# A GRU with a mixture of experts behind it: two gates in one PSUM bank, made by matmuls of 256 columns

## The chip, the core and the metric

The kernel runs on one core of a Trainium2 chip. Its time is the device time of one execution in microseconds (us); lower is better. The runs before the change took 1448.86, 1452.12 and 1456.24 us, so the median is 1452.12 us. One further execution was recorded by the hardware profiler; it took 1449.96 us, and all readings of the profile below are of that execution. Engines are named as in the profile: PE is TensorE's matmul, PEld its weight load, DVE is VectorE, ACT is ScalarE, POOL is GpSimd, SP is SyncE.

## What is computed

`x` is (8, 256, 512): 8 sequences of 256 steps with 512 features. A GRU runs over the steps, and its states go through a mixture-of-experts layer; `x` is added at the end. Everything is float32.

```python
def cell(h, x):                       # h: (8, 512), once for each of 256 steps
    gi = x @ W_ih + b_ih              # W_ih, W_hh: (512, 3 * 512)
    gh = h @ W_hh + b_hh
    i_r, i_z, i_n = jnp.split(gi, 3, axis=-1)
    h_r, h_z, h_n = jnp.split(gh, 3, axis=-1)
    r = jax.nn.sigmoid(i_r + h_r)
    z = jax.nn.sigmoid(i_z + h_z)
    n = jnp.tanh(i_n + r * h_n)
    h_new = (1.0 - z) * n + z * h
    return (h_new, h_new)
...
# the states of all steps, as 2048 tokens
topk_w, topk_ids = jax.lax.top_k(softmax(tokens @ w_gate), 2)     # 8 experts, weights normed
routed = sum over the two chosen experts of  w * (silu(g) * u) @ w_down[e]
shared = (silu(g) * u) @ w_sh_down                                # for every token
out = x + routed + shared
```

## The kernel before

**Blocks and steps.** The 256 steps are 16 blocks (`NB`) of `TS` = 16 steps. Step `n` needs the state of step `n - 1`, so the recurrence is a chain of 256 steps. TensorE's other work is cut into pieces and put between the steps: the projections of `x` for later blocks (`project`, tile `gip`), the shared expert for blocks that are done (`shared_unit`, tiles `gu_s` and `po`), and the routing. The routed experts (`tile_unit`) come behind the last step, when it is known which tokens each expert has.

**One step (`step`).** A gate's values lie as 4 groups of 8 partitions (8 sequences each), with 128 columns. Three PSUM banks, `ps_r`, `ps_n` and `ps_z`, hold one gate each in their first 128 columns. A bank is first filled ("opened", `open_gate`, line 458) by ScalarE: it copies the input's share of the gate, which lies ready in `seeds` or `seeds_n`, into the bank. The matmuls then add `h @ W_hh` to it (line 478): for each gate 4 row blocks `q` of the state times 4 column groups `j`, 16 matmuls of 128 columns each. A float32 matmul stands in the profile as two passes, so a gate is 32 of them.

VectorE turns each gate by a transpose of 32x32 squares (`turned`, line 489), which also moves it out of PSUM. The order of the work of one step is the order of the lines:

- VectorE turns r; ScalarE takes its sigmoid (line 493) and opens r's bank for the next step (458);
- VectorE turns n and multiplies (496); ScalarE opens n's bank (458); VectorE adds the input's share of n (498); ScalarE takes the tanh (500);
- VectorE turns z; ScalarE takes its sigmoid (502) and opens z's bank;
- VectorE makes the new state in three operations (505, 507, 508), the last of which (`hT`) is what the next step's matmuls wait for; ScalarE keeps a copy of the state (511).

Every engine runs its own instructions in the order in which they are written. The waits between engines are set by a framework from the tiles that an instruction reads and writes.

**What stands between the steps.** After each step the loop over `t` calls the routing work that is due, then `catch_up(room)`, which runs work for VectorE from the list `afterwards` as far as 1.1 us (`WINDOW`) reach, and then takes pieces for TensorE from `queue` until the step's share of the block's work is done.

**x's turn.** `load_x(k)` brings a block of x by 8 loads on SP. `transpose_x(k)` turns it on VectorE (line 313) into `xT` for the projections and loads the next block behind that. Its place is set in the list of projections: a piece without work, put behind the projection of gate number 1 of a block, puts the turn of the next block into `afterwards`:

```python
for g in range(3):
    projections.extend(project(k, g))
    if g == 1 and k + 1 < NB:
        projections.append(Piece(lambda _: None, lambda k=k: turn_x_afterwards(k + 1), parts=0))
```

If a projection comes up before its turn has been run, the turn is run at once. Six pieces of this list are run before step 0, and `catch_up` behind them.

After the last step the three banks serve as `spare` for transposes of the routed experts.

Of the kernel before, what the change touches and what calls it, by code (L numbers as in the profile page):

```python
# [9 lines left out]
F32 = mybir.dt.float32  # L10
# [7 lines left out]
P = 128  # L18
# [7 lines left out]
def kernel(  # L26
# [52 lines left out]
    nc = tc.nc  # L79
    B, T, D = x.shape  # L80
# [4 lines left out]
    NQ = D // P  # L85
    NB = T // TS
# [16 lines left out]
    ps_gru = ctx.enter_context(tc.tile_pool(name="ps_gru", bufs=1, space=PSUM))  # L103
# [32 lines left out]
    whh = we[:, E - 4 : E - 2].rearrange("p e w n -> p (e w n)").rearrange("p (q n) -> p q n", q=NQ)  # L136
# [56 lines left out]
    seeds = [const.tile([P, SC, 2 * P], F32, name=f"seeds_{i}") for i in range(NS)]  # L193
# [6 lines left out]

    banks = {g: ps_gru.tile([P, D], F32, name=f"ps_{g}") for g in "rnz"}
    for bank in banks.values():
        nc.tensor.matmul(
            bank[:, 0:P], seeds[0][:, 0, 0:P], seeds[0][:, 0, 0:P], start=True, stop=True
        )
    xT_of = {}

    def turn_x_plain(k):  # L210
# [29 lines left out]
    def counting(name, n, base, step, channel):  # L240

        i = const.tile([P, n], I32, name=f"{name}_i")
        nc.gpsimd.iota(i, [[step, n]], base=base, channel_multiplier=channel)
        f = const.tile([P, n], F32, name=name)
        nc.vector.tensor_copy(f, i)
        return f
# [143 lines left out]
    def project(k, g):  # L390

        box = {}

        def issue(q, cols):
            if q == 0 and cols.start == 0:
                if k in turned_x:
                    turned_x.pop(k)()
                box["ps"], _ = bank_of([P, D], f"gip_{k}_{g}")
            multiply(
                box["ps"][:, cols],  # L400
                lambda c: xT_of[k][:, c, q, :],
                wih[:, q, g * D + cols.start : g * D + cols.stop],
                start=(q == 0 and cols.start == 0),
                stop=(q == NQ - 1 and cols.stop == D),
            )

        def by_group(t_):
            return t_.rearrange("p (q j i) -> p j q i", q=NQ, j=4)

        def end():  # L410
            to_gi = gi[:, :, g, :].rearrange("p j (q i) -> p j q i", q=NQ)
            bias_g = by_group(bias[:, g * D : (g + 1) * D])
            if k == 0:
                nc.vector.tensor_tensor(to_gi, by_group(box["ps"]), bias_g, ALU.add)
            else:
                nc.scalar.copy(to_gi, by_group(box["ps"]))
                nc.gpsimd.tensor_tensor(to_gi, to_gi, bias_g, ALU.add)
            if g > 0:
                to = gi_dram[k][g % 2].rearrange("j b t n -> (b t) j n")
                projected.add((k, "rzn"[g]))  # L420
                by = nc.sync if k else nc.scalar
                if g == 1:
                    by.dma_start(to.rearrange("p j (a n) -> p j a n", a=2), gi[:, :, 0:2, :])
                else:
                    by.dma_start(to, gi[:, :, 2, :])

        return [
            matmul_piece(lambda cols, q=q: issue(q, cols), end if q == NQ - 1 else None)
            for q in range(NQ)
        ]  # L430
# [4 lines left out]
    def load_seeds(c, of="nz"):  # L435

        k, o = divmod(c * SC, TS)
        steps = slice(o, o + SC)
        for g in of:
            assert (k, g) in projected  # L440
            tile_, at_row, src = (
                (seeds_n[c % NS], B, gi_dram[k][0]) if g == "n" else (seeds[c % NS], 0, gi_dram[k][1])
            )
            for j in range(4):
                by = nc.sync if c else nc.scalar
                row = 32 * j + at_row
                by.dma_start(tile_[row : row + B], src[j, :, steps, :])

    def open_gate(n, g):

        if n >= T:
            return
        c, t = divmod(n, SC)
        if g == "n":
            src = seeds_n[c % NS][:, t]
        else:
            src = seeds[c % NS][:, t].rearrange("p (a n) -> p a n", a=2)[:, "rz".index(g)]
        nc.scalar.copy(banks[g][:, 0:P], src)  # L458

    whh_v = whh.rearrange("p q (a k j i) -> p q a j k i", a=3, k=NQ, j=4)  # L460
    hc_of = {}

    def hc_of_block(k):
        return hc_of[k // 2][:, NG * (k % 2) : NG * (k % 2) + NG]
# [5 lines left out]
    def step(n):  # L470
        k, t = divmod(n, TS)
        c, ts = divmod(n, SC)
        hT, new = states[n % NH], states[(n + 1) % NH][:, :, 0:B]
        for g, bank in banks.items():
            a = "rzn".index(g)
            for q in range(NQ):
                for j in range(4):
                    nc.tensor.matmul(  # L478
                        bank[32 * j : 32 * j + B, 0:P].rearrange("b (k i) -> b k i", k=NQ),
                        hT[:, q, 0:B],  # L480
                        whh_v[:, q, a, j, :],
                        start=False,
                        stop=(q == NQ - 1),
                        skip_group_check=True,
                    )

        def turned(g):
            gT = turned_gates[g]
            nc.vector.transpose(gT.rearrange("p a b -> p (a b)"), banks[g][:, 0:P])  # L489
            return gT  # L490

        r = turned("r")[:, :, 0:B]
        nc.scalar.activation(r, r, AF.Sigmoid)  # L493
        open_gate(n + 1, "r")
        nT = turned("n")
        nc.vector.tensor_tensor(r, nT[:, :, 0:B], r, ALU.mult)
        open_gate(n + 1, "n")
        nc.vector.tensor_tensor(r, nT[:, :, B : 2 * B], r, ALU.add)  # L498
        nn = r
        nc.scalar.activation(nn, nn, AF.Tanh)  # L500
        z = turned("z")[:, :, 0:B]
        nc.scalar.activation(z, z, AF.Sigmoid)
        open_gate(n + 1, "z")

        nc.vector.tensor_tensor(hn, hT[:, :, 0:B], nn, ALU.subtract)  # L505
        nc.gpsimd.tensor_copy(last_hn, hn[:, 0, 0:1])  # L506
        nc.vector.tensor_tensor(z, z, hn, ALU.mult)
        nc.vector.tensor_tensor(new, nn, z, ALU.add)  # L508
        if t == 0 and k % 2 == 0:
            hc_of[k // 2] = two.tile([P, 2 * NG, NQ, 32], F32, tag="hc", name=f"hc_{k // 2}")  # L510
        nc.scalar.copy(  # L511
            hc_of_block(k).rearrange("p g q (c t) -> p q g c t", t=TS)[:, :, :, :, t],
            new.rearrange("p q (g c) -> p q g c", c=2),
        )
# [406 lines left out]
    for k in range(1, NB):  # L921
        for g in range(3):
            projections.extend(project(k, g))
            if g == 1 and k + 1 < NB:
                projections.append(
                    Piece(lambda _: None, lambda k=k: turn_x_afterwards(k + 1), parts=0)
                )

    def turn_x_afterwards(k):
        turned_x[k] = afterward(1.1, lambda: transpose_x(k))  # L930
# [3 lines left out]
        projections.popleft().run(None)  # L934
    catch_up(None)
    load_seeds(1)
    for g in banks:
        open_gate(0, g)
    for k in range(NB):

# [38 lines left out]
        for t in range(TS):  # L979
            n = k * TS + t  # L980
            step(n)
            if (n + 1) % SC == 0 and n + 1 < T and (n + 1) // SC + NS - 1 < T // SC:
                load_seeds((n + 1) // SC + NS - 1)
            room = WINDOW
            for cost, busy, work in at.get(t, ()):
                work()
                spent += cost
                room -= busy
            catch_up(room)
            if loads and (k < 2 or k == NB - 1 or t % 2):  # L990
                loads.popleft()()

            due = all_of_it * (t + 1) / TS
            while queue and (queue[0].left() == 0 or due - spent >= 0.5 * queue[0].cost):
                spent += queue[0].run(due - spent)
                if queue[0].left() == 0:
                    queue.popleft()
# [4 lines left out]
    k = NB - 1  # L1002
# [75 lines left out]
```

## Time and profile before

| | |
|---|---|
| median of 3 runs | 1452.12 us (1448.86 to 1456.24) |
| the profiled execution | 1449.96 us, its span 1448.1 us |
| mean granted TensorE clock | 0.991 |
| steps of the recurrence | from 36.1 to 1180.3 us of the span |
| r's, n's, z's matmuls (L478) | 8192 passes each, busy 291.8, 293.0 and 292.3 us |
| a gate's turn (L489) | 256 each, 317 ns |
| opening r's bank (L458, ACT) | 256, 262 ns |
| r's sigmoid (L493, ACT) | 256, 229 ns |
| x's turn (L313, DVE) | 14, 1143 ns |

A row of the profile names the line, the engine, the operation, what it writes and reads, and the shape; then the busy time, the mean of one, and the idle time of the engine just before it with what ended that. In a timeline the columns are the start in the span, the duration, the engine, the line and the operation; rows of several instructions (x32) reach from the start of the first to the end of the last. A row of the stretches ("windows") has the stretch, its length, the busy time of PE, PEld, DVE, ACT and POOL with the number of instructions, then the granted clock, the busy share of the DMA engines and GB/s.

### The profile page before, as it was taken

The page shows a single profiled execution, that of the slowest core. Times are in us where ns is not written, and L with a number is a line of the kernel's source. Part 1 is how long each engine was busy: PE and PEld are TensorE (multiplying, and loading weights), DVE is VectorE, ACT ScalarE, POOL GpSimd, SP SyncE. Part 2 cuts the span into 40 slices and gives each one's busy share as a digit, 9 for nine tenths or more (in the row PEclk, how much of TensorE's full clock was granted, in tenths as well). Part 3 has the DMA queues.
Part 4 walks back from the last instruction along what each step waited for, and adds up shares of the span by engine and source line. Part 5 has one row for each costly group of instructions (what it writes and reads, how often), then busy time and mean ns, then how long its engine had stood idle before and what let it go on. Part 6 is the DMA issues. An engine that isn't in the chain of part 4 may idle for free.

```text
span 1448.1 us, 75006 instructions
## 1 busy us (share of the span) xinstructions
PE 1398.4 (97%) x33084; PEld 1064.6 (74%) x33084; DVE 683.3 (47%) x2661; ACT 496.2 (34%) x2072; POOL 284.9 (20%) x525
## 2 busy tenths in 40 slices
PE   5999999999999999999999999999999999999995
PEld 2677778886788888889887878888887864444442
DVE  2445445544555555555545554555455552222221
ACT  0433333433333434343433333334343420222221
POOL 1333321111111101010101010101010222344442
PEclk9999999999999999999999999999999999999998
DMA  7334422122212021111011111111111424444453
GB/s 262 96 118 101 72 73 61 56 65 65 58 54 48 15 51 30 36 45 37 29 40 29 40 45 35 32 34 27 32 45 37 98 62 117 90 93 88 89 91 46
DMA packets 66949, 91.97 MB, mean 64 GB/s; under 512 B 12688, under 2 KB 44480, under 8 KB 66624
## 3 DMA queue, kind: packets, MB, share of 16 engines
q0 software_dynamic: 15104, 37.57, 12.4%
q1 hardware_dynamic: 50176, 48.60, 12.3%
q8 instruction: 261, 4.28, 1.3%
q10 hardware_dynamic: 1344, 1.00, 0.2%
q14 instruction: 64, 0.52, 0.1%
HBM read 56.80 MB, written 30.32 MB: 60 GB/s over the span
## 4 chain that ended last, share of the span: by engine, by line
PE 94%; DMA 2%; DVE 1%; issue 1%; POOL 0%; ACT 0%; DVEq 0%; SPq 0%; POOLq 0%; ACTq 0%
PE ps_r L478 16%; PE ps_n L478 16%; PE ps_z L478 15%; PE gu_s L768 15%; PE gip L324 10%; PE gu_t L722 8%; PE po L324 7%; PE yp L853 4%; DMA gid_rz<-gi 1%; DMA x<-in_x_dram 0%; DMA we<-in_L_cond_b_hh_dram 0%; PE ps_z L833 0%; PE ps_r L833 0%; PE ps_n L833 0%; DMA out_dram<-y,row 0%
## 5 line engine op out<-in xcount | busy, mean ns | idle before, releaser
L478 PE MATMUL ps_r<-we,hT 128*8 128x128 f32 x8192 | 291.8, 273 | 11.4 <-ACT ps_r L458 8.9
L478 PEld LDWEIGHTS ps_r<-we,hT 128*8 128x8 f32 x8192 | 242.8, 90 | 79.2 <-ACT ps_z L458 25.3
L478 PE MATMUL ps_n<-we,hT 128*8 128x128 f32 x8192 | 293.0, 273 | 5.0 <-issue 5.0
L478 PE MATMUL ps_z<-we,hT 128*8 128x128 f32 x8192 | 292.3, 273 | 3.0 <-issue 3.0
L768 PE MATMUL gu_s<-hc,wsu 128*32 128x256 f32 x4096 | 260.5, 379 | 1.2 <-issue 1.1
L478 PEld LDWEIGHTS ps_n<-we,hT 128*8 128x8 f32 x8192 | 240.3, 90 | 8.4 <-issue 6.6
L478 PEld LDWEIGHTS ps_z<-we,hT 128*8 128x8 f32 x8192 | 240.1, 90 | 5.8 <-issue 4.2
L506 POOL COPY last_hn<-hn 128x1 f32<-128x1 f32 x256 | 47.3, 185 | 905.0 <-DVE hn L505 902.7
L489 DVE STREAM_TRANSPOSE rT<-ps_r 128x128 f32<-128x128 f32 x256 | 81.2, 317 | 304.4 <-PE ps_r L478 304.3
L324 PE MATMUL gip<-we,xT 128*32 128x512 f32 (+3 forms) x2080 | 195.8, 489 | 7.2 <-DVE xT L313 5.4
L768 PEld LDWEIGHTS gu_s<-hc,wsu 128*32 128x32 f32 x4096 | 161.0, 110 | 52.0 <-issue 7.8
L493 ACT ACTIVATE rT<-rT 128x32 f32<-128x32 f32 x256 | 58.6, 229 | 374.8 <-DVE rT L489 374.8
L489 DVE STREAM_TRANSPOSE nT<-ps_n 128x128 f32<-128x128 f32 x256 | 81.3, 317 | 149.4 <-PE ps_n L478 149.4
L324 PE MATMUL po<-wsd,act_s 128*32 128x512 f32 (+3 forms) x1304 | 135.7, 501 | 0.7 <-DVE again L806 0.7
L722 PE MATMUL gu_t<-we,xrT 128*128 x280 | 131.6, 593 | 0.3 <-issue 0.3
L324 PEld LDWEIGHTS gip<-we,xT 128*32 128x32 f32 x2080 | 76.4, 111 | 69.3 <-issue 56.4
L458 ACT COPY ps_n<-seeds_n 128x128 f32<-128x128 f32 x256 | 69.0, 269 | 110.8 <-DVE nT L489 107.7
L511 ACT COPY hc<-hT 128x32 f32<-128x32 f32 x256 | 63.2, 247 | 88.1 <-DVE hT L508 87.4
L489 DVE STREAM_TRANSPOSE zT<-ps_z 128x128 f32<-128x128 f32 x256 | 81.2, 317 | 13.0 <-PE ps_z L478 3.9
L500 ACT ACTIVATE rT<-rT 128x32 f32<-128x32 f32 x256 | 58.7, 229 | 68.3 <-DVE rT L498 68.2
L324 PEld LDWEIGHTS po<-wsd,act_s 128*32 128x32 f32 x1304 | 52.2, 110 | 38.2 <-issue 27.4
L859 POOL DMA_INDIRECT out_dram<-y,row x35 | 55.5, 1586 | 112.8 <-DVE y L856 108.9
(164 smaller groups left out, 1193.9 us busy)
## 6 DMA issues: line engine op xcount, KB each, us to landing
we<-in_L_ffn_w_gate_up_dram POOLq DMA_DIRECT2D x32, 256.0 KB, 3.9
seeds<-gid_rz SPq DMA_DIRECT2D x252, 32.0 KB
gid_rz<-gi SPq DMA_DIRECT2D x15, 512.0 KB
wsu<-_L_ffn_w_sh_gate_up_dram POOLq DMA_DIRECT2D x16, 256.0 KB, 3.3
rows<-hr SPq DMA_DIRECT2D x128, 32.0 KB
we<-in_L_ffn_w_down_dram POOLq DMA_DIRECT2D x16, 256.0 KB, 4.5
again<-in_x_dram SPq DMA_DIRECT2D x16, 256.0 KB
out_dram<-again SPq DMA_DIRECT2D x16, 256.0 KB
```

Of the source, the lines that this page charges most:

```text
L324: nc.tensor.matmul(ps[32 * c : 32 * c + 32], lhs(c), rhs, start=start, stop=stop, skip_group_check=True,)
L458: nc.scalar.copy(banks[g][:, 0:P], src)
L478: nc.tensor.matmul(bank[32 * j : 32 * j + B, 0:P].rearrange("b (k i) -> b k i", k=NQ), hT[:, q, 0:B], whh_v[:, q, a, j, :], start=False, s ...
L489: nc.vector.transpose(gT.rearrange("p a b -> p (a b)"), banks[g][:, 0:P])
L493: nc.scalar.activation(r, r, AF.Sigmoid)
L500: nc.scalar.activation(nn, nn, AF.Tanh)
L506: nc.gpsimd.tensor_copy(last_hn, hn[:, 0, 0:1])
L511: nc.scalar.copy(hc_of_block(k).rearrange("p g q (c t) -> p q g c t", t=TS)[:, :, :, :, t], new.rearrange("p q (g c) -> p q g c", c=2),)
L722: nc.tensor.matmul(box["ps"], lhs(q), w_up(q), start=(q == 0), stop=(q == NQ - 1))
L768: nc.tensor.matmul(box["ps"][32 * g : 32 * g + 32, two_i, :], wsu[c][:, q, two_i, fs], hc_of[m][:, :, q, :], start=(two_i == 0 and q == 0) ...
L853: nc.tensor.matmul(box["y"], lhs, rhs, start=(f == 0), stop=(f == NF - 1))
L859: nc.gpsimd.indirect_dma_start(out=out.rearrange("b t d -> (b t) d"), out_offset=bass.IndirectOffsetOnAxis(ap=laid["row"][:, i : i + 1], a ...
```

## The change

r and n now share one bank, `ps_rn`: r in columns 0 to 127, n in columns 128 to 255. One matmul makes both, with 256 columns: the weights of r and n are taken together by a slice with a step of two gates. Each step has 16 matmuls of 256 columns and 16 of 128 (z) in place of 48 of 128. The opening, the turns and all that follows stay separate for r and n and stand in the same order as before. A third bank, `ps_x`, takes the place of the bank that came free; it is used for transposes behind the last step. Apart from that, x's turn is put behind the projection of gate number 0 in place of number 1.

```diff
-    banks = {g: ps_gru.tile([P, D], F32, name=f"ps_{g}") for g in "rnz"}
+    banks = {g: ps_gru.tile([P, D], F32, name=f"ps_{g}") for g in ("rn", "z", "x")}
     for bank in banks.values():
         nc.tensor.matmul(
-            bank[:, 0:P], seeds[0][:, 0, 0:P], seeds[0][:, 0, 0:P], start=True, stop=True
+            bank[:, 0 : 2 * P], seeds[0][:, 0, 0:P], seeds[0][:, 0], start=True, stop=True
         )
+    gate_of = {"r": banks["rn"][:, 0:P], "n": banks["rn"][:, P : 2 * P], "z": banks["z"][:, 0:P]}
...
-        nc.scalar.copy(banks[g][:, 0:P], src)
-
-    whh_v = whh.rearrange("p q (a k j i) -> p q a j k i", a=3, k=NQ, j=4)
+        nc.scalar.copy(gate_of[g], src)
+
+    whh_v = whh.rearrange("p q (a k j i) -> p q j a k i", a=3, k=NQ, j=4)
...
-        for g, bank in banks.items():
-            a = "rzn".index(g)
+        for g, gates in (("rn", slice(0, 3, 2)), ("z", slice(1, 2))):
+            n_ = len(g)
             for q in range(NQ):
                 for j in range(4):
                     nc.tensor.matmul(
-                        bank[32 * j : 32 * j + B, 0:P].rearrange("b (k i) -> b k i", k=NQ),
+                        banks[g][32 * j : 32 * j + B, 0 : n_ * P].rearrange(
+                            "b (a k i) -> b a k i", a=n_, k=NQ
+                        ),
                         hT[:, q, 0:B],
-                        whh_v[:, q, a, j, :],
+                        whh_v[:, q, j, gates],
                         start=False,
                         stop=(q == NQ - 1),
                         skip_group_check=True,
                     )
...
-            nc.vector.transpose(gT.rearrange("p a b -> p (a b)"), banks[g][:, 0:P])
+            nc.vector.transpose(gT.rearrange("p a b -> p (a b)"), gate_of[g])
...
-            if g == 1 and k + 1 < NB:
+            if g == 0 and k + 1 < NB:
                 projections.append(
                     Piece(lambda _: None, lambda k=k: turn_x_afterwards(k + 1), parts=0)
                 )
...
-    for g in banks:
+    for g in gate_of:
         open_gate(0, g)
```

In the instructions of the changed kernel the waits of a step stand as follows (engine, instruction, what it waits for), where the count of ScalarE is the one that the copy of r's seeds reaches:

```
PE    Matmult ps_rn<-we,hT           VectorE (hT) and ScalarE
DVE   StreamTranspose rT<-ps_rn      TensorE
ACT   Activation rT<-rT              VectorE
ACT   TensorCopy ps_rn<-seeds        TensorE
DVE   StreamTranspose nT<-ps_rn      ScalarE (TensorCopy ps_rn<-seeds)
ACT   TensorCopy ps_rn<-seeds_n      VectorE
```

In the kernel before, `nT<-ps_n` waited for TensorE.

## The prediction

> **What bounds the kernel now.** I read the page first, then the stages, then one step as a timeline, then TensorE's waits.
>
> ```profile
> PE 1398.4 (97%) x33084; PEld 1064.6 (74%) x33084; DVE 683.3 (47%) x2661; ACT 496.2 (34%) x2072; POOL 284.9 (20%) x525
> ...
> PE 94%; DMA 2%; DVE 1%; issue 1%; POOL 0%; ACT 0%; DVEq 0%; SPq 0%; POOLq 0%; ACTq 0%
> ```
>
> TensorE (PE) looks like the only bound: busy 97% of the span, and 94% of the chain that ended last. But the ends of matmuls are modelled, so this doesn't say how far the recurrence is behind it. For that one needs the time of a step. The stretches of the run:
>
> ```profile
> 36.10:412.00 375.90, 359.91 (x9747) 285.71 (x9748) 184.49 (x749) 140.96 (x612) 90.20 (x169) 0.99 0.29 76
> 412.00:1114.20 702.20, 701.34 (x19927) 595.85 (x19925) 381.28 (x1568) 276.49 (x1222) 76.62 (x202) 1.00 0.14 37
> 1114.20:1180.30 66.10, 65.32 (x1932) 54.13 (x1924) 36.25 (x154) 25.54 (x116) 11.70 (x31) 1.00 0.30 70
> ```
>
> These hold the 256 steps: blocks 0 to 4 (80 steps, 4.70 us each, with stalls), blocks 5 to 14 (160 steps, 4.39 us each), block 15 (16 steps, 4.13 us each). What comes behind 1180.3 us has no step in it. Now one ordinary step, from its first r matmul at 820.52 to the next one's at 824.87 (columns: start, duration, engine, line, operation):
>
> ```profile
> 820.52 1.07 PE L478 MATMUL ps_r<-we,hT 128*8 128x128 f32 x32
> ...
> 821.39 1.06 PE L478 MATMUL ps_n<-we,hT 128*8 128x128 f32 x32
> 821.65 0.32 DVE L489 STREAM_TRANSPOSE rT<-ps_r 128x128 f32<-128x128 f32 x1 [0.75 <-PE ps_r L478]
> 822.06 0.23 ACT L493 ACTIVATE rT<-rT 128x32 f32<-128x32 f32 x1 [1.67 <-DVE rT L489]
> ...
> 822.19 0.26 ACT L458 COPY ps_r<-seeds 128x128 f32<-128x128 f32 x1
> 822.27 1.07 PE L478 MATMUL ps_z<-we,hT 128*8 128x128 f32 x32
> 822.52 0.32 DVE L489 STREAM_TRANSPOSE nT<-ps_n 128x128 f32<-128x128 f32 x1 [0.56 <-PE ps_n L478]
> ...
> 822.94 0.19 DVE L496 TENSOR_TENSOR rT<-nT,rT 128x32 f32<-128x32 f32 x1
> ...
> 823.14 1.92 PE L768 MATMUL gu_s<-hc,wsu 128*32 128x256 f32 x32
> 823.16 0.19 DVE L498 TENSOR_TENSOR rT<-nT,rT 128x32 f32<-128x32 f32 x1
> 823.39 0.32 DVE L489 STREAM_TRANSPOSE zT<-ps_z 128x128 f32<-128x128 f32 x1
> ...
> 823.74 0.23 ACT L502 ACTIVATE zT<-zT 128x32 f32<-128x32 f32 x1
> ...
> 824.02 0.19 DVE L507 TENSOR_TENSOR zT<-zT,hn 128x32 f32<-128x32 f32 x1
> 824.25 0.19 DVE L508 TENSOR_TENSOR hT<-rT,zT 128x32 f32<-128x32 f32 x1
> ...
> 824.87 0.30 PE L478 MATMUL ps_r<-we,hT 128*8 128x128 f32 x4
> ```
>
> The reader should see two chains side by side. TensorE: r, n, z, then one portion of other work (gu_s), then the next r: 4.35 us without a gap. The recurrence: n's last matmul ends at 821.39+1.06 = 822.45, n is turned at 822.52, L496 follows at 822.94, the new state (L508) ends at 824.44, which is 3.92 us into the step. r's turn, its sigmoid and the refilling of r's bank (L458) lie wholly under n's and z's matmuls. How soon may the next r begin after the state? In the last block, where less other work is queued:
>
> ```profile
> 1146.72 0.19 DVE L508 TENSOR_TENSOR hT<-rT,zT 128x32 f32<-128x32 f32 x1
> ...
> 1147.06 1.06 PE L478 MATMUL ps_r<-we,hT 128*8 128x128 f32 x32
> ```
>
> 0.15 us behind it. So the recurrence alone needs 3.92 + 0.15 = 4.07 us for a step, and TensorE takes 4.35: **the room is 0.28 us per step.** A change of the order on VectorE and ScalarE that costs more than this comes out 256 times.
>
> **The change part by part.** (1) *32 matmuls per step in place of 48* (the profile has two passes of each, 64 against 96). Two groups of 128 columns take 821.39−820.52 = 0.87 us each, 1.74 together; the nearest row for 32 passes of 256 columns is gu_s, which reads its moving operand in runs of 32 too: 823.14 to the next r at 824.87, 1.73 us. That is about 0.02 us per step (19 ns by the unrounded starts), 256 × 0.019 = 4.9 us if TensorE is the bound. The Trainium skill ("TensorE: Matmul & The Clock Gate", section "Wait — 56ns, not 53.3ns?") would give more: a fixed cost of about 2.5 ns per warm matmul, 32 passes fewer are 80 ns, over 256 steps 20 us as an estimate. The trace shows a quarter of that here, where four column groups run at once; I take the trace. The weight loads that fall away run beside matmuls.
>
> (2) *r and n in one bank: the waits.* r can't be turned when its own 16 matmuls are done, only after all of rn. And the two engines that touch the bank now take turns. In the changed kernel's program r's turn waits for TensorE, and n's turn waits on ScalarE's count, at the value that the refilling of r (the copy ps_rn<-seeds right behind r's sigmoid) reaches; before, n's turn waited for TensorE alone. The bank's users run one after the other although their columns differ. Queued behind the waiting turn on VectorE are L496, L498, z's turn and the rest of the step; the next rn matmul waits for them all. I follow one step with the rows above, from the first rn matmul:
> - rn's last matmul ends at 1.92 (gu_s row), r's turn starts at 1.98 (0.06 to 0.07 behind, as above).
> - r's sigmoid 0.41 later, 2.39; the refilling 0.13 later, 2.52, and it ends at 2.78.
> - n's turn: a VectorE instruction that waits for ScalarE. The nearest row is L507, which starts 0.05 behind z's sigmoid (823.97 to 824.02). So 2.83, ending at 3.15. Its bounds are 0.02 and 0.10.
> - L496 behind it: 0.03, as L498 stands behind L496 (before it was 0.10, with two waits; I keep that as the upper end). 3.18, against 2.42 before.
> - L496 to the end of L508: 824.44−822.94 = 1.50 as before, since z's turn already started when L498 ended. 4.68; and 0.15 to the next matmul: **4.83 us.**
>
> So the recurrence grows by 0.76 us, the room takes 0.28, and TensorE stands about 0.5 us in each step. The Trainium skill ("PSUM — Partial Sum Buffer", section "PSUM bank collisions raise a hardware error") speaks against this change in the same place: semaphores should guard a bank and 32-partition quadrant, not addresses, so two column ranges of one bank are no two buffers. Without the rule's wait n's turn would start right behind r's, see the second rival; with it the step is 4.83. The trace of before, with a bank to each gate, can't show which; the program's wait decides.
>
> (3) *The third bank* ("x") is used only behind the steps, like n's before: nothing. The three first matmuls have 256 columns: under 0.3 us, before the inputs are there.
>
> (4) *x's turn queued one projection earlier.* Same 14 turns on VectorE (1.15 us each) and the same 8 loads on SP behind each. Gain:
>
> ```profile
> PE gip L324 <- DVE xT L313: 5.4, 2, 3.4
> ```
>
> TensorE waits twice for xT, 2.0 us near 125 and 3.4 us near 350. In the changed order the turn comes 14 steps ahead of the second use, but still in the same step as the first: −3.4 us. What it is moved past: the first turn now stands before step 0, on VectorE, which idles there until 38.09; its x is issued by 33.9, so 0 to 1 us. On SP the next 8 loads (5.8 us of issue in the trace, 44.4 to 50.2) go ahead of the seeds of chunk 1, issued at 34.0 before and needed about 54: hidden; in some blocks they go ahead of a gid_rz store, whose readers come a block later: nothing, and a few us at most if that cover were gone.
>
> **The sum.** Blocks 5 to 14: 160 × 4.83 − 702.2 = +70.6. Block 15: 16 × 4.83 − 66.1 = +11.2. Blocks 0 to 4: by the steps' starts 65 of 80 lie below 4.83 and rise to it, +26.7; 15 are longer (instruction fetch, routing work on VectorE, xT) and stay; less 3.4 for (4): +23.3. Ends: +7 if the longer pace swallows those stalls, +34 if they add to it. Together +105. The profiled execution took 1449.96 us (span 1448.1), so 1555; the median of the runs, 1452.12, is 2.2 us above it: **1557 us.**
>
> **The rivals.**
> *TensorE covers it (faster).* With PE at 97% one may hold that only TensorE's work counts: −4.9 − 3.4 (to −5.4) us, 1442 to 1444, 0.6 to 0.7% faster. It decides where the recurrence grows by less than the 0.28 us of room. For it: the page. Against: r's turn alone starts 0.85 us later (1.98 against 1.13), and with the refilling in front of n's turn 0.76 arrive at L496. 2 in 100.
> *The wait costs nothing (same).* If n's turn follows r's directly, 1.98+0.32+0.02 = 2.32, it ends at 2.64; r's sigmoid ends at 2.62, L496 starts at 2.68, 0.26 later than before: 4.33 us per step, just inside the room. The short steps rise by some 8 us, (1) and (4) give as much back: 1449 to 1455. For it: disjoint columns. Against: the wait stands in the program. 3 in 100.
> *The clock falls as well (much slower).* One window shows it:
>
> ```profile
> 353.00:360.00 7.00, 7.00 (x139) 4.32 (x135) 1.91 (x8) 1.33 (x7) 0.18 (x1) 0.77 0.19 50
> ```
>
> 0.77 is the granted clock behind the 3.4 us that TensorE stood for xT. At that clock rn takes 2.5 us, a step 5.4, the run about 1700. But a stand of 0.5 us in 4.83 is far shorter than 3.4. 2 in 100.
>
> **How the numbers follow.** 93 in 100 for the serialised bank at 1557, 2 for it with the lower clock, 3 for no wait, 2 for the cover. The range: a step of 4.78 with the stalls swallowed gives +63 +10 +13 = about 1538; 4.92 with the stalls added +85 +13 +40 = 1590, of which I cut the last few: 1538 to 1584. About 0.5% is what a measurement of this kernel can tell from no change. Slower has 0.95 (the first two cases), the same 0.03, faster 0.02.
>
> **What would show it.** In the profile after: steps of 4.83 us (160 steps from 412 on before now take some 773); n's turn with its idle time put down to ScalarE's refilling of ps_rn; PE busy near 90%, and its matmul on ps_rn idle for VectorE's hT, over 100 us in all; 32 rn passes in a row of 1.9 us; the wait for xT down by 3.4. I am wrong if n's turn starts within 0.4 us of r's turn, if the steps stay at 4.35, or if the clock row falls below 0.9 in the middle of the run.

## The result and the profile after

The changed kernel takes 1551.12 us (median of 4 runs, 1550.3 to 1551.84), the kernel before 1450.49 us (median of 4, 1447.03 to 1456.24). The ratio is 1.069, with a 95% interval of 1.0652 to 1.0726: slower by about 100 us. The prediction was 1557 us. The profiled execution of the changed kernel took 1551.47 us, its span is 1549.6 us, 101.5 us longer than before.

From the page of the changed kernel: the engines, the instruction queue, the chain that ended last by engine, and two groups of section 5 (busy time, mean ns of one, then the idle time of the engine just before them and what ended it).

```profile
PE 1431.2 (92%) x24884; PEld 793.9 (51%) x24884; DVE 660.0 (43%) x2661; ACT 490.6 (32%) x2072; POOL 285.0 (18%) x525
...
q8 instruction: 197, 3.23, 0.9%
...
PE 55%; DVE 20%; ACT 14%; issue 5%; DMA 4%; ACTq 0%; SPq 0%; POOL 0%; DVEq 0%; POOLq 0%
...
L479 PE MATMUL ps_rn<-we,hT 128*8 128x256 f32 x8192 | 492.3, 381 | 89.7 <-DVE hT L511 67.9
...
L492 DVE STREAM_TRANSPOSE nT<-ps_rn 128x128 f32<-128x128 f32 x256 | 81.1, 317 | 137.0 <-ACT ps_rn L459 137.0
```

The last row is the change in one line: n's turn has 137.0 us of idle time before it, and all of it is put down to ScalarE's opening of `ps_rn` (line 459). In the kernel before (called "before" from here on) the same row was

```profile
L489 DVE STREAM_TRANSPOSE nT<-ps_n 128x128 f32<-128x128 f32 x256 | 81.3, 317 | 149.4 <-PE ps_n L478 149.4
```

VectorE's idle time there was no shorter; what has changed is what ends it, and how late in the step. VectorE and ScalarE have not become busier (660.0 and 490.6 us, less than before), yet the chain that ended last went from 94% PE to 55% PE, 20% DVE and 14% ACT. The bound of the steps is no single engine any more, it is a path across three of them. The number of TensorE's matmul passes has fallen by a quarter (33084 to 24884) and the instruction queue brings 3.23 MB in place of 4.28; both come up again below.

The stretches of the changed kernel, cut as those of before at the end of the state of step 80, 240 and 256:

```profile
36.87:431.80 394.93, 366.87 (x7188) 205.39 (x7188) 176.24 (x748) 139.30 (x612) 89.38 (x169) 0.99 0.27 71
431.80:1205.80 774.00, 726.77 (x14800) 419.55 (x14801) 366.55 (x1567) 272.30 (x1222) 76.57 (x202) 1.00 0.12 32
1205.80:1282.90 77.10, 65.70 (x1420) 39.93 (x1424) 35.59 (x157) 25.71 (x118) 12.22 (x32) 1.00 0.24 59
```

In the middle one PE was busy for 701.34 of 702.20 us before; now it is busy for 726.77 of 774.00 at a granted clock of 1.00. One ordinary step of it, from rn's first matmul at 882.30 to the next at 887.10 (start, duration, engine, line, operation, and in brackets the idle time before it and what ended that):

```profile
882.30 1.91 PE L479 MATMUL ps_rn<-we,hT 128*8 128x256 f32 x32 [0.48 <-DVE hT L511]
884.02 1.06 PE L479 MATMUL ps_z<-we,hT 128*8 128x128 f32 x32
884.28 0.32 DVE L492 STREAM_TRANSPOSE rT<-ps_rn 128x128 f32<-128x128 f32 x1 [1.33 <-PE ps_rn L479]
884.68 0.23 ACT L496 ACTIVATE rT<-rT 128x32 f32<-128x32 f32 x1 [2.25 <-DVE rT L492]
884.82 0.26 ACT L459 COPY ps_rn<-seeds 128x128 f32<-128x128 f32 x1
884.90 1.92 PE L771 MATMUL gu_s<-hc,wsu 128*32 128x256 f32 x32
885.11 0.32 DVE L492 STREAM_TRANSPOSE nT<-ps_rn 128x128 f32<-128x128 f32 x1 [0.52 <-ACT ps_rn L459]
885.46 0.19 DVE L499 TENSOR_TENSOR rT<-nT,rT 128x32 f32<-128x32 f32 x1
...
886.77 0.19 DVE L511 TENSOR_TENSOR hT<-rT,zT 128x32 f32<-128x32 f32 x1
...
887.10 1.91 PE L479 MATMUL ps_rn<-we,hT 128*8 128x256 f32 x32 [0.29 <-DVE hT L511]
```

Read it down the brackets. r's turn waits for all of rn (884.28), the sigmoid for r's turn, the opening for the sigmoid, and n's turn for the opening: it starts 0.03 us behind the opening's end (885.08). Line 499, which stood 2.42 us into the step, stands 3.16 us into it. On TensorE the gu_s portion ends at 886.82, and the next rn comes at 887.10: TensorE stands idle for 0.29 us, put down to `hT`; ahead of this step it was 0.48. (Such an idle time of TensorE is called a stand below.)

The same lengths for every kernel that follows, counted between the ends of steps' states:

| from the end of one step's state to another's, us | 1 to 80 | 80 to 240 | 240 to 256 | span |
|---|---|---|---|---|
| before | 370.7 | 701.8 | 66.7 | 1448.1 |
| after | 388.6 | 773.9 | 76.8 | 1549.6 |
| x's turn alone | 363.6 | 704.0 | 67.0 | 1444.1 |
| shared bank alone, x's turn as before | 396.4 | 773.0 | 76.9 | 1557.5 |
| n's turn ahead of the opening | 356.0 | 702.3 | 69.2 | 1438.3 |
| two banks in turns | 354.1 | 702.3 | 69.3 | 1435.7 |
| one bank, 128 columns | 401.7 | 779.7 | 77.2 | 1569.2 |
| two banks, 128 columns | 368.6 | 709.5 | 70.3 | 1459.4 |
| two banks, x's turn still earlier | 352.1 | 702.2 | 69.3 | 1434.3 |
| opening r twice | 412.3 | 822.1 | 81.4 | 1626.7 |
| two banks, 128 columns, later loads | 364.1 | 713.9 | 70.4 | 1459.1 |

After less before is +17.9, +72.1 and +10.1 us; with +1.9 for the first step and −0.5 behind the last, that is the 101.5.

### The profile page after: what moved, and what is told of

Read it like the earlier page. It is cut to its first block, busy times and chain, and to the rows that moved or that the text cites. A ratio compares the mean times of both kernels' runs of the same rounds, so it can differ in the third digit from the quotient of the medians.

```text
span 1549.6 us, 58344 instructions
## 1 busy us (share of the span) xinstructions
PE 1431.2 (92%) x24884; PEld 793.9 (51%) x24884; DVE 660.0 (43%) x2661; ACT 490.6 (32%) x2072; POOL 285.0 (18%) x525
## 3 DMA queue, kind: packets, MB, share of 16 engines
q8 instruction: 197, 3.23, 0.9%
## 4 chain that ended last, share of the span: by engine, by line
PE 55%; DVE 20%; ACT 14%; issue 5%; DMA 4%; ACTq 0%; SPq 0%; POOL 0%; DVEq 0%; POOLq 0%
PE ps_rn L479 31%; PE gu_t L725 8%; DVE nT L492 4%; DVE rT L492 4%; PE gu_s L771 4%; PE yp L856 4%; ACT rT L503 3%; ACT zT L505 3%; ACT ps_rn L459 3%; PE po L325 3%; DVE rT L499 3%; DVE rT L501 3%; DVE hT L511 3%; DVE zT L510 3%; ACT rT L496 2%
## 5 line engine op out<-in xcount | busy, mean ns | idle before, releaser
L479 PE MATMUL ps_rn<-we,hT 128*8 128x256 f32 x8192 | 492.3, 381 | 89.7 <-DVE hT L511 67.9
L479 PEld LDWEIGHTS ps_rn<-we,hT 128*8 128x8 f32 x8192 | 217.0, 89 | 389.4 <-ACT ps_z L459 218.3
L479 PE MATMUL ps_z<-we,hT 128*8 128x128 f32 x8192 | 273.1, 273 | 0.0
L492 DVE STREAM_TRANSPOSE rT<-ps_rn 128x128 f32<-128x128 f32 x256 | 81.3, 317 | 431.2 <-PE ps_rn L479 431.2
L771 PEld LDWEIGHTS gu_s<-hc,wsu 128*32 128x32 f32 x4096 | 135.7, 110 | 67.3 <-issue 6.7
L492 DVE STREAM_TRANSPOSE nT<-ps_rn 128x128 f32<-128x128 f32 x256 | 81.1, 317 | 137.0 <-ACT ps_rn L459 137.0
L459 ACT COPY ps_rn<-seeds_n 128x128 f32<-128x128 f32 x256 | 68.9, 269 | 98.4 <-DVE nT L492 94.2
L716 DVE TENSOR_TENSOR act_t<-gu_t,act_t 128x256 f32<-128x256 f32 x35 | 14.9, 425 | 131.4 <-ACT act_t L712 131.4
L418 POOL TENSOR_TENSOR gi<-gi,bias 128x512 f32<-128x512 f32 x45 | 57.4, 1275 | 54.9 <-ACT gi L417 54.8
L459 ACT COPY ps_rn<-seeds 128x128 f32<-128x128 f32 x256 | 67.1, 262 | 0.2
```

The costliest lines, as they stand in the source:

```text
L459: nc.scalar.copy(gate_of[g], src)
L479: nc.tensor.matmul(banks[g][32 * j : 32 * j + B, 0 : n_ * P].rearrange("b (a k i) -> b a k i", a=n_, k=NQ), hT[:, q, 0:B], whh_v[:, q, j, ...
L492: nc.vector.transpose(gT.rearrange("p a b -> p (a b)"), gate_of[g])
L771: nc.tensor.matmul(box["ps"][32 * g : 32 * g + 32, two_i, :], wsu[c][:, q, two_i, fs], hc_of[m][:, :, q, :], start=(two_i == 0 and q == 0) ...
```

## The experiments

Each ratio below is to the kernel before as it ran beside that experiment. Its median there lay between 1455.61 and 1460.02 us, not at the 1450.49 of above, so kernels of different experiments are compared by their ratios.

### Which part of the change costs: x's turn alone, the shared bank alone

Before, with the place of x's turn changed and nothing else:

```diff
-    if g == 1 and k + 1 < NB:
+    if g == 0 and k + 1 < NB:
```

> The kernel before with x's turn alone moved (behind projection 0 in place of 1); banks and matmuls as before. Theory (the serialised bank makes the whole loss): the steps stay at 4.35 us, the wait of TensorE for xT near 350 us goes (3.4 us), that near 125 us stays; time 3 to 5 us under before, so 0.2 to 0.4% faster, within what can be told from no change. Rival (the moved turn and its eight loads hold up VectorE or SP's queue and make part of the loss): 5 us or more over before.

Measured: 1448.04 us, ratio 0.9946 (95% interval 0.9926 to 0.9965, and so below). The opposite, the changed kernel with that line put back to `g == 1`:

> The changed kernel with x's turn back behind projection 1: one bank for r and n and matmuls of 256 columns alone. Theory: steps of 4.81 us as in the changed kernel, time 1551 to 1556, ratio to before 1.069 to 1.073. Rival (x's turn has a part in the loss): clearly under 1545.

Measured: 1556.16 us, ratio 1.0685 (1.0655 to 1.0714), with a median step of 4.809 us as in the changed kernel. So the whole loss is that of the shared bank, and x's turn is a small gain. TensorE's wait for xT, two of 5.4 us together in before, became one in x's turn alone:

```profile
PE gip L324 <- DVE xT L313: 3.2, 1, 3.2
```

It is the early one, which grew from 2.0 to 3.2 us, and the late one of 3.4 us fell away. What such a stand can cost beyond its own length is seen in the stretches behind it, here of the kernel with the shared bank alone (the length, the busy times of five engines, then granted clock, DMA share and GB/s), where the late stand is 4.2 us:

```profile
372.00:376.00 4.00, 0.04 (x4) 0.00 (x0) 3.22 (x14) 1.52 (x8) 0.69 (x2) 0.83 0.45 137
376.00:380.00 4.00, 3.71 (x20) 1.04 (x24) 0.14 (x1) 0.00 (x0) 0.00 (x0) 0.50 0.39 96
380.00:384.00 4.00, 4.00 (x80) 2.24 (x76) 0.88 (x4) 0.66 (x3) 0.00 (x0) 0.82 0.05 15
```

Behind the stand TensorE works for 4 us at a clock of 0.50 and for 4 us at 0.82, which costs 2.0 + 0.7 us more. The prediction had counted the waits alone. But not every stand is followed by this: in the traces the lower clock comes as a stretch of 3.4 or 6.8 us at 0.50. One of 3.4 us follows xT's wait of 3.4 us in before; none follows its wait of 2.0 us there, and none a wait of 3.6 us for xT in the kernel with two banks below.

### Which step of the shared bank costs: n's turn ahead of the opening

The changed kernel with one line moved, so that VectorE's turn of n stands ahead of ScalarE's opening of r's columns. Nothing of the computation changes.

```diff
+        nT = turned("n")
         open_gate(n + 1, "r")
-        nT = turned("n")
```

> The changed kernel with two lines swapped: n's turn is issued ahead of the refilling of r's columns, so that VectorE turns r and n one after the other and ScalarE refills both behind that. One bank and 256 columns stay. Theory (n's turn behind ScalarE's refilling is what costs): n's turn starts 0.3 us or less behind r's, L499 waits for r's sigmoid at 2.66 us into the step in place of 3.16, the recurrence needs 4.31 to 4.33 us, TensorE 4.33; time 1446 to 1455, no difference from before that can be told. Rival (the late r and the wide matmuls cost, not the wait): steps stay over 4.7 us, time over 1530.

Measured: 1438.82 us, ratio 0.9878 (0.9857 to 0.99). One step of it:

```profile
804.02 1.92 PE L479 MATMUL ps_rn<-we,hT 128*8 128x256 f32 x32
...
806.00 0.32 DVE L492 STREAM_TRANSPOSE rT<-ps_rn 128x128 f32<-128x128 f32 x1 [1.53 <-PE ps_rn L479]
806.24 0.28 DVE L492 STREAM_TRANSPOSE nT<-ps_rn 128x128 f32<-128x128 f32 x1
806.41 0.23 ACT L496 ACTIVATE rT<-rT 128x32 f32<-128x32 f32 x1 [1.75 <-DVE rT L492]
806.60 0.27 ACT L459 COPY ps_rn<-seeds 128x128 f32<-128x128 f32 x1
806.67 0.19 DVE L499 TENSOR_TENSOR rT<-nT,rT 128x32 f32<-128x32 f32 x1 [0.16 <-ACT rT L496]
...
807.98 0.19 DVE L511 TENSOR_TENSOR hT<-rT,zT 128x32 f32<-128x32 f32 x1
...
808.34 0.62 PE L479 MATMUL ps_rn<-we,hT 128*8 128x256 f32 x8
```

n's turn now follows r's by 0.24 us, and line 499 waits for the sigmoid, 2.65 us into the step. The step is 4.32 us here, 4.29 the shortest of the run. The 100 us were the order of two instructions in one bank, and all of them come back. That r's turn still waits for all of rn puts line 499 0.23 us later than in before (2.65 and 2.42), which is less than the room of 0.28: the middle stretch is as long as before (702.3 and 701.8 us). Only in the last block, where TensorE has less other work, does it show: 69.2 us in place of 66.7.

### The same by space in place of order: two banks in turns

The bank of rn alternates by the step between `ps_rn` and the bank `ps_x` that stood empty during the steps; the order of lines is that of the changed kernel.

```diff
-    gate_of = {"r": banks["rn"][:, 0:P], "n": banks["rn"][:, P : 2 * P], "z": banks["z"][:, 0:P]}
+    rn_of = (banks["rn"], banks["x"])
+
+    def gate_at(n, g):
+        if g == "z":
+            return banks["z"][:, 0:P]
+        return rn_of[n % 2][:, slice(0, P) if g == "r" else slice(P, 2 * P)]
...
```

> The changed kernel with the idle third bank used: odd steps make r and n in one bank, even steps in the other, so that the refilling for the next step never touches the bank that is being turned. Order of the lines as in the changed kernel. Theory: no wait of n's turn for ScalarE; recurrence 4.31 to 4.33 us as with the swapped lines, TensorE 4.33; time 1445 to 1453. Rival (sharing a bank costs nothing, it is r's lateness): over 1530. A time clearly under that with the swapped lines would say that the refilling behind n's turn still held something up there.

Measured: 1438.0 us, ratio 0.9878 (0.9857 to 0.9899), with the same offsets within the step as in the experiment before. Two unlike edits that both take ScalarE's write out from between the two turns give the same time. (The wait is one that the framework put into the program. No kernel here shares the bank in the old order without it, so what the hardware would do then isn't shown.) Neither was expected to beat before by 1.2%, though: with the recurrence back inside TensorE's time, the prediction's sum leaves only the shorter matmuls and x's turn. The table says where it comes from: 701.8 and 702.3 us in the middle stretch, so nothing there, but 356.0 and 354.1 against 370.7 in the first.

### The price of the wait, measured by doubling it

The changed kernel, opening r's columns twice in a row with the same data:

```diff
         open_gate(n + 1, "r")
+        open_gate(n + 1, "r")
```

> The changed kernel, but ScalarE refills r's columns twice with the same values. The second copy starts behind the end of the first, 0.26 + 0.04 = 0.30 us later. Theory (n's turn waits for the end of the refilling, and the step for n's turn): every step gets 0.30 us longer, 4.81 to 5.11, 256 x 0.30 = 77 us more, time 1620 to 1632. Rival (the refilling is only where the wait is booked, something else on the path ends later): less than 30 us more.

Measured: 1628.15 us, ratio 1.1164 (1.1129 to 1.12). A step is 5.109 us, 0.300 more than in the changed kernel:

```profile
900.22 0.56 ACT L459 COPY ps_rn<-seeds 128x128 f32<-128x128 f32 x2
900.82 0.32 DVE L492 STREAM_TRANSPOSE nT<-ps_rn 128x128 f32<-128x128 f32 x1 [0.82 <-ACT ps_rn L459]
```

The two openings take 0.56 us, n's turn follows at once, and its idle time went from 0.52 to 0.82 us. The whole 0.300 us arrives in every step, so the opening lies on the path with its full length.

### What the wide matmul is worth: 128 columns, in one bank and in two

The changed kernel with r's matmuls and n's separate again, in the halves of the same bank; then the two-bank version with the same edit.

```diff
-        for g, gates in (("rn", slice(0, 3, 2)), ("z", slice(1, 2))):
+        for g, at_, gates in (("rn", 0, slice(0, 1)), ("rn", P, slice(2, 3)), ("z", 0, slice(1, 2))):
...
```

> The changed kernel (x's turn moved too) with r and n in one bank as there, but made by 128-column matmuls again, all of r's and then all of n's: the shared bank without the wide matmul. Theory (the shared bank is the loss, not the width): r's turn waits for n's matmuls too (1.93 us), n's turn for the refilling, steps of 4.81 to 4.83 us, time 1549 to 1562. Rival (the 256-column matmuls end r late and so make the loss): r's turn again at 1.13 us and steps near 4.35 to 4.5, time under 1490.

Measured: 1570.48 us, ratio 1.078 (1.0743 to 1.0817), 8 us over the upper end of what was expected. The step is 4.830 us, 0.021 longer than with the wide matmul, which agrees with the 19 ns of the prediction and makes 160 × 0.021 = 3.4 us of the 5.8 in the middle stretch. In the first stretch it is 13.1 us slower than the changed kernel, and its waits put down to "issue" (explained below) are 8.6 us there in place of 0.3. That r's matmuls end earlier here helps nothing: r's turn starts at 1.995, as late as with the wide matmul, since it waits for all that goes into the bank.

> The kernel with two alternating banks, but with 128-column matmuls, r's and then n's, in the bank of the step: the same chain and the same waits as with the two banks, and 48 matmuls per step in place of 32. It tells what the wide matmul itself gives. Theory A (fewer instructions to fetch for TensorE): besides 20 ns on each step that TensorE limits, blocks 0 to 4 take 6 us or more longer again (near 368 us where two wide banks took 360), with TensorE's waits put down to issue back; time 1446 to 1452. Theory B (only the 20 ns per step): blocks 0 to 4 stay within 3 us of those of the two wide banks, time 1440 to 1444.

Measured: 1462.3 us, ratio 1.0024 (1.0005 to 1.0044), against 0.9878 for two banks with the wide matmul: 0.0146, 21 us. Both theories are off, Theory A by 10 us and Theory B by more. The spans differ by 23.7 us, of which 14.5 lie in the first stretch, while the waits for xT are the same (3.6 us, once). What differs is a kind of wait that the profile calls "issue": TensorE waited for nothing that the profile names. From the waits of PE between 190 and 445 us with two banks and 128 columns (total us, times, longest):

```profile
PE ps_rn L484 <- issue: 2.4, 1, 2.4
PE lgp L533 <- issue: 1.6, 1, 1.6
PE gu_s L776 <- issue: 0.5, 2, 0.3
PE ps_z L484 <- issue: 0.4, 1, 0.4
```

and between 110 and 440 us with two banks and the wide matmul:

```profile
PE ps_rn L485 <- issue: 0.4, 1, 0.4
PE ps_z L485 <- issue: 0.2, 1, 0.2
```

Between 110 and 190 us the first has another 2.6 us of them. In the whole run it is about 9 us against less than 1; before had 10.5, and the changed kernel 0.6. The kernels with 48 matmuls per step have about 75000 instructions and 4.28 MB in the instruction queue, those with 32 about 58500 and 3.23 MB.

Do these stands wait for instructions? The traces hold every transfer of the instruction queue (q8): 261 of 16 KB with 48 matmuls, 197 with 32, in both cases 65 bytes for each of TensorE's matmul passes and weight loads, one in 4.7 us of the steps or one in 6.2 us. Three issue waits of over 1 us with two banks and 128 columns, against the transfer that landed last before each ended (us of the span):

| transfer starts | lands | TensorE stands from | goes on at |
|---|---|---|---|
| 147.10 | 151.70 | 150.44 | 152.66 |
| 193.68 | 194.62 | 194.46 | 196.03 |
| 237.32 | 238.90 | 238.00 | 240.36 |

All profiles here together have 49 issue waits of over 0.5 us between 50 and 1300 us of the span, every one in a kernel with 48 matmuls. 46 of them end between 0.95 and 1.62 us behind the landing of such a transfer. Of the 360 waits of that length that are put down to something else, 42 do. So these stands are, as far as the traces can tell, waits for a block of instructions. Why a block comes late isn't settled: one of the three transfers took 4.6 us where the median is 1.1, the other two 0.9 and 1.6.

By the steps, 19 of the 79 in the first stretch differ by more than 0.2 us and make 12.8 of its 14.5 us. Of the 14.5, some 6.7 are the issue waits, 1.7 the lower clock behind the first of the three (0.50 for 3.4 us), and 1.7 the pace (79 × 0.021). The other 4 us stay open.

### Is it the weights' loading? The loads put later

In the first stretch the DMA engines also bring the experts' weights, which may hold up the instructions. Two banks with 128 columns, and 24 of the weight loads (experts 0 to 3) issued from block 8 on in place of block 2:

```diff
-        if k == 2:
+        if k == 8:
```

> The kernel with two alternating banks and 128-column matmuls, with one thing moved: the 24 weight loads (256 KB each) of experts 0 to 3 are issued in blocks 8 to 10 in place of blocks 2 to 4. In the narrow kernel TensorE stood 4.9 us in blocks 2 to 4 (190 to 440 us) in waits put down to issue. Theory (its instructions come late while the weight loads hold the DMA engines): under 1 us of such waits is left there, and as much or somewhat less comes up in blocks 8 to 10 (650 to 870 us); time within 5 us of the narrow kernel with two banks. Rival (the place in the program, with the routing's code, makes these waits): they stay in blocks 2 to 4.

Measured: 1465.97 us, ratio 1.0067 (1.0034 to 1.0101). PE's issue waits between 190 and 445 us fell from 4.9 to 1.7 us, not below 1 as expected; those left are

```profile
PE lgp L533 <- issue: 0.9, 1, 0.9
PE ps_rn L484 <- issue: 0.8, 1, 0.8
```

and between 620 and 890 us, where there had been 1.3 us, there are now

```profile
PE ps_z L484 <- issue: 3.1, 2, 1.6
PE ps_rn L484 <- issue: 0.2, 1, 0.2
```

The first stretch is 4.5 us shorter than without this edit, the middle one 4.4 us longer. So some 3 us of the waits left the place that the loads left, and 2.0 us more came where the loads came; over the whole run they are as many (8.9 us in both profiles). That speaks for the loads as one cause of late instructions. It is no proof: a part stayed, and such waits differ by some us between two executions of one kernel, as is seen below.

### The best version: x's turn still earlier

Two banks with the wide matmul, and x's turn put into VectorE's list with a smaller cost, so that it is run at once:

```diff
-        turned_x[k] = afterward(1.1, lambda: transpose_x(k))
+        turned_x[k] = afterward(0.1, lambda: transpose_x(k))
```

> The kernel with two alternating banks and 256 columns, where x's turn asks for 0.1 us of VectorE's room instead of 1.1, so that it runs at the next step that has any room. Expected: the turn for block 4 comes a step or two ahead of its first use, the remaining wait of TensorE for xT (3.6 us) goes, time 3 to 4 us under the two banks (1434 to 1436). Rival (the turn then runs into r's turn on VectorE and holds up the recurrence): no gain or a few us more.

Measured: 1433.9 us, ratio 0.9834 (0.9807 to 0.986). The wait for xT (3.6 us) is gone from PE's waits, though the first stretch is only 2.0 us shorter than with two banks. It is the fastest of the kernels here, 1.7% under before.

### How well x's turn is known: two runs on one chip

The kernel before, unchanged, and x's turn alone, once more:

> The kernel before, unchanged, to have a second profiled execution of it on the same chip as the next run. The x-turn-only kernel measured 7.9 us under before, although the profiled spans (1444.1 against 1448.1) show 4.0. Theory A: the profile of before was of one of its better executions; an ordinary one waits more for instructions. Then this profile has a span of about 1453 us and 13 to 16 us of issue waits on PE in place of 10.5, all before 440 us or in the middle of the run. Theory B: the profile was ordinary and chips differ by this much: a span near 1448 us on a chip where before's median is near 1450. The ratio to before has to hold 1.

> Before with x's turn behind the first projection of a block, once more, on one chip with a second profile of before. Theory A: again 6 to 9 us under before (ratio about 0.995), and its profile has one wait for xT of about 3.2 us and 5 to 8 us less of issue waits than the second profile of before. Theory B: 3 to 5 us under before (ratio about 0.997), and issue waits within 3 us of those of before.

Measured: the unchanged kernel 1463.51 us, ratio 1.0025 (1.0007 to 1.0043); x's turn alone 1454.09 us, ratio 0.9953 (0.9932 to 0.9974). The first number is a caution: two identical programs differ by a quarter of a per cent, and the interval doesn't hold 1, so 0.0024 for two banks with 128 columns is no difference from before. The second profile of before has a span of 1456.4 us and 13.4 us of issue waits (10.5 in the first), as Theory A said. In x's turn alone, with a span of 1454.4 us, the profile puts 16.6 us down to issue; the longest are

```profile
PE ps_n L478 <- issue: 4.2, 5, 3.1
PE gip L324 <- issue: 3.5, 2, 3.2
```

and names no wait for xT. But the 3.2 us of the second row are that wait under another name, as the timeline shows: the projection starts 0.15 us behind the end of x's turn, as it does in the first profile of this kernel.

```profile
135.36 1.08 DVE L313 STREAM_TRANSPOSE xT<-x 128x512 f32<-128x512 f32 x1
136.59 3.33 PE L324 MATMUL gip<-we,xT 128*32 128x512 f32 x16 [3.16 <-issue]
```

Without it 13.4 us are left, as many as in before. So the one wait for xT of about 3.2 us that Theory A expected is there, and the 5 to 8 us fewer of issue waits are not. With 48 matmuls per step these waits change from one execution to the next (7.6 and 13.4 us in two profiles of the same kernel), about as much as x's turn moves. Its size stays open: 6 to 9 us by medians beside before; 4.0, 7.9 and 2.0 us by three pairs of profiles; nothing measurable between the two kernels with the shared bank (1.0685 and 1.0689).

## Why the prediction was right, and where its terms were off

**The mechanism and the sum: right.** Slower with 0.95, 1557 us against 1551.12, within the range. The step from row to row, in us behind the first rn matmul:

| | predicted | measured (median of the steps) |
|---|---|---|
| r's turn starts | 1.98 | 1.974 |
| r's sigmoid starts | 2.39 | 2.385 |
| n's turn starts | 2.83 | 2.812 |
| line 499 starts (496 before) | 3.18 | 3.163 |
| state ends | 4.68 | 4.663 |
| next step | 4.83 | 4.809 |

The 0.02 that are missing enter at n's turn: VectorE starts 0.03 us behind the opening's end, where the row of line 507 had given 0.05. The blocks, in the cut of the stretches above: +70.6 predicted for 5 to 14, +71.8 measured (the mean step there is 4.84, as a few steps are longer than the chain); block 15 +11.2 and +11.0; blocks 0 to 4 +23.3 and +19.0.

**Blocks 0 to 4: a good sum from terms that were off.** The 65 short steps were to rise by 26.7 us. They did, by 32.0, but 4.9 of it is a single step that now holds the early wait for xT. The 15 long steps were to "stay", less 3.4 us for xT. They fell by 13.1: 4.6 with the late wait for xT and the lower clock behind it, 1.8 where the early wait moved out to the next step, and 6.7 for which the prediction had no term. Before had 9.3 us of issue waits in these blocks, the changed kernel 0.3. That the sum came within 4.3 us is in part luck: the early wait's growth and what the other stalls lost have opposite signs.

**The room of 0.28 us per step: right, and the reason why a loss of 0.74 came out as 0.46.** n's turn ahead of the opening shows it from the other side: 0.23 us, less than the room, cost nothing in the middle stretch.

**Rule against trace, twice.** The rule of the Trainium skill ("PSUM — Partial Sum Buffer", section "PSUM bank collisions raise a hardware error") that a bank and quadrant are guarded, not addresses, named the danger; the wait is there with 137.0 us of idle time, and both ways around it (order, second bank) remove it. For the matmul's fixed cost the prediction took the trace's 19 ns per step and not the 80 ns that the 2.5 ns per warm matmul of the Trainium skill ("TensorE: Matmul & The Clock Gate", section "Wait — 56ns, not 53.3ns?") would make, as an estimate: the two one-bank kernels differ by 21 ns per step, so the trace was the better guide for the pace of the matmuls.

**The term that was mis-sized: (1), the wide matmul.** "About 4.9 us if TensorE is the bound", and the weight loads that fall away "run beside matmuls". Two kernels with the same named waits differ by 21 us by ratios. The step's pace is a few us of that (0.021 us a step, 3.4 of the 7.2 us in the middle stretch); most of the rest is in the first stretch, where the issue waits fall from 7.3 to 0.6 us. The prediction named instruction fetch among the stalls of blocks 0 to 4, but let the stalls stay as they were, although the change takes away a quarter of TensorE's instructions. The gain is there in the changed kernel too: the one-bank kernel with 128 columns is slower than it by 13 us by ratios. It is also why the two repaired versions are 1.2% faster than before where "the same" had been expected of them: with 128 columns the version with two banks is not (1.0024).

**(4), x's turn: −3.4 us, measured between 0 and 9.** The wait that went is the one named. Left out was the clock behind the stand: the prediction itself showed 7 us at 0.77 after it, which is 1.6 us more. Also unforeseen was that the early stand grows: from 2.0 to 3.2 us in x's turn alone and to 3.8 us in the changed kernel. (The eight loads behind a turn take 6.3 us of issue, 44.40 to 50.71; the 5.8 of the prediction are seven of them. Nothing hangs on it.)

**The rivals.** TensorE's cover decides below 0.28 us of growth and there were 0.74. The free wait was described with n's turn at 2.32 and a step of 4.33: that is what n's turn ahead of the opening gives (2.22 and 4.29 to 4.33), so the rival was the right picture of another order of lines, only not of this one. Its time of 1449 to 1455 was again too high, by the wide matmul's term. The clock didn't fall in the middle of the run: 1.00 in the row of 431.80 to 1205.80, with a stand of some 0.3 to 0.5 us in an ordinary step.

**What would show it.** n's turn put down to ScalarE: yes. Busy share of PE near 90%: 92%. rn row of 1.9 us: 1.91. The wait for xT down by 3.4 us: no, from 5.4 to 3.8, as the late one went and the early one grew. Idle for `hT` over 100 us: no. PE's waits name

```profile
PE ps_rn L479 <- DVE hT L511: 67.9, 183, 1.1
```

that is, 183 of 256 steps. The loss counted by the steps is 100 us; the ends of matmuls are modelled and fill part of the stand, so the length of a step is the surer measure than an idle time of PE.

## What to carry to other kernels

Before two buffers are merged into one bank, write down who reads and writes the bank in program order. Under this framework a write between two reads became a wait for the second reader, though the columns differ, and it cost what it exceeded the room by, once per step. Here one line moved (read both, then refill) or a second bank in turns turned the loss of 6.9% into a gain of 1.2% over before, and with x's turn early 1.7%. And count instructions as a resource of their own: the wide matmul was worth some four times what its matmul time said (21 us against 4.9).

## What the runs showed of the hardware that was not expected

- The number of instructions has a price in time. With the same named waits, 48 matmuls per step in place of 32 (4.28 against 3.23 MB of instructions) cost 21 us of 1438, with single issue waits of up to 2.4 us. In all profiles together, 46 of 49 such waits of over 0.5 us end 0.95 to 1.62 us behind the landing of a 16 KB transfer of the instruction queue; why the transfers are late isn't shown, though part of the waits moved with the weight loads.
- "Issue" in a profile can hide a named wait: 3.16 us of it in one profile of x's turn alone are the wait for xT, which another profile of the same kernel names.
- A VectorE turn that doesn't depend on the one before starts before that one's end: 806.24 behind 806.00 with 0.32 us of duration, so 0.24 us apart and 0.08 us overlapped.
- The length of a stand alone doesn't tell the clock behind it. In before a stand of 2.0 us for xT (to 131.1) left it at 1.00, and one of 2.0 us for instructions (to 158.1) was followed by 3.4 us at 0.50. Of two stands of 3.6 us for xT, the one with two banks left it at 1.00, the one with n's turn ahead of the opening was followed by 6.8 us at 0.50. Stands of some 0.3 to 0.5 us in each step left it at 1.00.
